# Two-layer masked attention: the closing turns and the opening's weight sums in another order

## The chip, the core and the metric

The kernel runs on one core of a Trainium2 chip. Its engines are TensorE (PE in the profile), VectorE (DVE), ScalarE (ACT), GpSimd (POOL) and SyncE (SP), which here issues all the transfers. Each engine works through its own queue of instructions in order, and waits by semaphores for what others must have done. The metric is the device time of one execution in microseconds (us).

## What is computed

The input x has 128 graphs of 128 nodes with 512 features, adj is a boolean mask for each graph. Two attention layers follow one another, each with a residual and a layer norm:

```python
# layer 0: 4 heads of 64
q, k, v = (split_heads(x @ W) for W in (Wq, Wk, Wv))
sim = where(adj, einsum(q, k) * 64 ** -0.5, -float32_max)
x = layernorm(x + einsum(softmax(sim), v) @ Wo + bo)
# layer 1: 8 heads of 64
h = (x - mean(x)) * rsqrt(var(x) + 1e-5) * gamma + beta
q, k, v = split(h @ w_qkv.T)
sim = where(adj | eye, einsum(q, k) * 64 ** -0.5, -1e9)
x = layernorm(x + einsum(softmax(sim), v) @ w_out.T + b_out)
```

All arithmetic is float32.

## The kernel before, in words

Graphs are taken in groups of two (G = 2), 64 groups in all (NG). The order of all instructions is written out by hand (`tc.manual_schedule()`, line 49): there is no scheduler, so the order of the calls in the functions is the order in every engine's queue. Pools of named tiles decide only which earlier use an instruction has to wait for.

The work is a software pipeline. A turn s of `step` (L819) makes for group s the first layer's q, k and v (`product_0`, L437), for group s-1 its scores and softmax, for s-2 its attention, output product and norm. For the second layer it makes q, k and v of group s-3 (`product`, called as `qk` and `v`), the softmax of s-4, and the attention, output product and norm of s-5. `opening` (L781) does turns 0 and 1, `step` runs for s = 2 to 63, `closing` for s = 64, 65 and 66, and `last` is turn 67.

Matrix products are made as seven block products in place of eight (numbered 1 to 7; the order is mostly 1, 2, 6, 5, 7, 3, 4). Three accumulation banks in PSUM, "a", "c" and "f", take them (`INTO`, L307). Products 1, 6, 7 and 4 all add into "a", so between two of them the partial result is read out: by ScalarE for 1, 6 and 5 (`tap`, L344, the copies `ev`, `eqk`, `e`), by VectorE with an add for 2, 7 and 3, and by ScalarE for 4. Each later product in the same bank waits for that read. In `out_product` (L476) every product is added to the residual rows `r` by VectorE (L501), and a next product in the same bank waits for that add.

The block products need sums of weight blocks, made once: `weight_sums` (L173) and `combine` (L182), four subtractions for each block, on VectorE but for one block of w1qk. They need sums of input blocks too: `halves_sums` (L296), four GpSimd operations for each group (`xs` of the input, `so` of the attention result).

A product wants the input with its features on the partitions. `turn` (L224) does that by way of DRAM: VectorE turns 32x32 blocks (L229), SP stores them (`scr`, L214), `arrive` (L233) fetches them with four transfers (`raw`, L220), and ScalarE puts them in order: `in_order` (L250) for layer 0, `finish` (L259), which applies gamma and beta, for layer 1. The probabilities go the same way: `normalised` (L582: a reciprocal on VectorE, a multiplication on GpSimd), `blocks` (L600: VectorE, then a store `scrp`), `probs_arrive` (L612: four fetches `pT`). In the opening and in the last turn `transposed` and `blocks_direct` (L621) have TensorE turn them instead. `finish_direct` (L274) would do so for the second layer's input; in the kernel before nothing calls it.

The softmax is `scores` (TensorE), `masked` (VectorE copies the scores under the mask into a tile that GpSimd has cleared), `maxima` (VectorE), `exps` (ScalarE, eight per part) and `normalised`. Part 0 is layer 0, parts 1 and 2 are the two graphs of layer 1. `attend` (L635) is probabilities times v, followed by a ScalarE copy (`aT`). `stats` (L684) makes mean and variance on VectorE, small GpSimd operations turn them into scale and shift, and the norms on ScalarE (L724) are put off to the next `flush()`. `addend` (L672) scales the residual rows on ScalarE (layer 1) and adds the bias on GpSimd (L679). `with_self` (L540) joins the diagonal to the mask. For the first two and the last three groups (`PLAIN_QK`) q and k of layer 1 are made with the features on the partitions at once.

Of the kernel before, what the change touches and what calls it, by code (L numbers as in the profile page):

```python
# [27 lines left out]
def kernel(ctx: ExitStack, tc: tile.TileContext, x, adj, wq, wk, wv, wo, bo,  # L28
                            gamma, beta, w_qkv, w_out, b_out, out):
    nc = tc.nc  # L30
    B, N, E = x.shape
    KC = E // P
    NG = B // G
# [136 lines left out]
    wsqk = const.tile([P, 3, KH, I1], F32, name="wsqk")  # L170
    wsv = const.tile([P, 3, KH, I1 // 2], F32, name="wsv")

    def weight_sums(w, ws, *blocks_):  # L173

        for c in blocks_:
            h0, h1 = (1, 0) if w is w1qk else (0, 1)
            b11, b12 = w[:, c, h0], w[:, c, h1]
            b21, b22 = w[:, KH + c, h0], w[:, KH + c, h1]
            combine(b11, b12, b21, b22, ws[:, 0, c], ws[:, 1, c], ws[:, 2, c],
                    eng=nc.gpsimd if w is w1qk and c == 0 else nc.vector)  # L180

    def combine(b11, b12, b21, b22, t2, t3, t4, eng=nc.vector):  # L182

        for o, a, b in ((b12, b12, b11), (t2, b22, b12), (t3, t2, b11), (t4, b21, t2)):
            eng.tensor_tensor(o, a, b, op=ALU.subtract)

    def weight_sums_0():
# [319 lines left out]
    PARTS = (0, 1, 2)  # L507
# [2 lines left out]
        g = s - (4 if part else 1)  # L510
        return g if 0 <= g < NG else None

    def scores(s):

        made = {}
        for part in PARTS:
# [302 lines left out]
    def step(s):  # L819

        made = scores(s)
        load_ahead(s + 1)
        if s > 2:
            in_order(s)
        if s > 3:
            sums(0, s)
        arrive(1, s - 3)
        flush()
        load_rows(s - 1)
        masked(made, s, 0, 1, 2)  # L830
        attend(s)
        maxima(s, 0, 1)
        out_sums(0, s - 2)
        if s == 3:
            sums(0, s)
        exps(s, 0, 0)
        product_0(s, 1)
        exps(s, 0, 1)
        out_product(0, s - 2, 1, 2, 5)
        maxima(s, 2)  # L840
        product_0(s, 2)
        normalised(s, 0)
        out_product(0, s - 2, 6, 3)
        exps(s, 1, 0)
        stats(0, s - 2, 0)
        if s == 2:
            turn(0, s + 1)
            arrive(0, s + 1)
        product_0(s, 6)
        exps(s, 1, 1)  # L850
        out_product(0, s - 2, 7)
        (blocks_direct if s == 2 else blocks)(s, 0)
        product_0(s, 5)
        out_product(0, s - 2, 4)
        normalised(s, 1)
        finish(s - 3, 0)
        stats(0, s - 2, 1)
        exps(s, 2, 0)
        product_0(s, 7)
        finish(s - 3, 1)  # L860
        exps(s, 2, 1)
        blocks(s, 1)
        product_0(s, 3)
        if s > 2:
            turn(0, s + 1)
        product_0(s, 4)
        if s in (2, 3):
            prepare(len(setup) - (s == 2))
        normalised(s, 2)
        if s == 3:  # L870
            weight_sums(w1v, wsv, 0, 1)
        qk(s - 3, 1)
        if s == 2:
            weight_sums(w1qk, wsqk, 1)
            prepare(1)
        flush()
        if s > 2:
            probs_arrive(s, 0, 1)
        qk(s - 3, 2)
        blocks(s, 2)  # L880
        qk(s - 3, 6, 5)
        flush(latest)
        addend(1, s - 5)
        out_sums(1, s - 5)
        qk(s - 3, 7, 3, 4)
        q_arrive(s - 3)
        k_arrive(s - 3)
        probs_arrive(s, 2)
        if s > 2:
            arrive(0, s + 1)  # L890
        out_product(1, s - 5, 1, 2)
        v(s - 3, 1, 2)
        turn(1, s - 2)
        cleared(s + 1, 0, 1, 2)
        v(s - 3, 6)
        out_product(1, s - 5, 6, 5)
        v(s - 3, 5)
# [8 lines left out]
        with_self(s - 2)  # L906
        if s == 3:
            weight_sums_out(1)
        if s == NG - 1:
            arrive(1, s - 2)  # L910

    def closing(s):

        chunks = [lambda p=p, i=i: exps(s, p, i) for p in PARTS if group_of(s, p) is not None
                  for i in range(2)]

        def some():
            if chunks:
                chunks.pop(0)()

        made = scores(s)
        flush()
        load_rows(s - 1)
        finish(s - 3, 0)
        masked(made, s, 0, 1, 2)
        attend(s)
        maxima(s, 0, 1)
        out_sums(0, s - 2)
        finish(s - 3, 1)
        out_product(0, s - 2, 1, 2)  # L930
        if s == NG + 2:
            addend(1, s - 5)
            out_sums(1, s - 5)
            out_product(1, s - 5, 1, 2)
        some()
        qk(s - 3, 1)
        maxima(s, 2)
        out_product(0, s - 2, 5, 6)
        some()
        qk(s - 3, 2)  # L940
        out_product(0, s - 2, 7, 3)
        if s == NG + 2:
            out_product(1, s - 5, 5, 6)
        some()
        qk(s - 3, 6)
        out_product(0, s - 2, 4)
        normalised(s, min(s - NG, 1))
        stats(0, s - 2, 0)
        stats(0, s - 2, 1)
        some()  # L950
        qk(s - 3, 5)
        blocks(s, min(s - NG, 1))
        some()
        qk(s - 3, 7)
        if s == NG:
            normalised(s, 1)
        some()
        flush()
        turn(1, s - 2)
        if s == NG + 2:  # L960
            normalised(s, 2)
            blocks(s, 2)
            probs_arrive(s, 1, 2)
            out_product(1, s - 5, 7, 3, 4)
        else:
            addend(1, s - 5)
            out_sums(1, s - 5)
        qk(s - 3, 3, 4)
        if s < NG + 2:
            if s == NG:  # L970
                blocks(s, 1)
            normalised(s, 2)
            out_product(1, s - 5, 1, 2)
            blocks(s, 2)
            probs_arrive(s, 0, 1, 2)
            arrive(1, s - 2)
            v(s - 3, 1, 2, 6)
            out_product(1, s - 5, 6, 5)
            v(s - 3, 5)
            out_product(1, s - 5, 7, 3, 4)  # L980
            v(s - 3, 7, 3, 4)
        flush(latest)
        stats(1, s - 5, 0)
        stats(1, s - 5, 1)
        cleared(s + 1, 0, 1, 2)
        addend(0, s - 1)
        with_self(s - 2)

    def last():
# [2 lines left out]
        made = scores(s)  # L992
        masked(made, s, 1)
        maxima(s, 1)
        v(s - 4, 1, 2, 6)
        exps(s, 1, 0)
        attend(s)
        flush()
        masked(made, s, 2)
        maxima(s, 2)  # L1000
        addend(1, s - 5)
        exps(s, 1, 1)
        out_product(1, s - 5, 1, 2)
        exps(s, 2, 0, 1)
        out_sums(1, s - 5)
        normalised(s, 1)
        addend(1, s - 4)
        v(s - 4, 5)
        out_product(1, s - 5, 6, 5)
# [20 lines left out]
    opening()  # L1030
    for s in range(2, NG):
        step(s)
    for s in range(NG, NG + 3):
        closing(s)
    last()


# [27 lines left out]
```

## Time and profile before

| what | us |
|---|---|
| median of 3 runs (2791.12 to 2794.29) | 2791.74 |
| the profiled execution | 2794.32 |
| its span | 2792.5 |
| TensorE busy | 2748.1 (98%) |
| VectorE busy | 1950.3 (70%) |
| GpSimd busy | 1748.8 (63%) |
| ScalarE busy | 1528.3 (55%) |
| share of TensorE in the chain of waits that ended last | 94% |
| turn 62, scores to scores (a steady turn) | 42.4 |
| turn 3 / turn 4 | 39.5 / 38.4 |
| turns 64, 65, 66 | 40.6, 40.3, 34.6 |
| from the scores of turn 67 to the end | 42.5 |

Times in the profile count from the start of the span. TensorE's busy time includes matmuls whose ends are modelled and overlap their successors, so what counts is the distance between starts. In a list of waits, the bracket at the end of a line gives the engine's idle time before that instruction and what ended it.

### The profile page before, as it was taken

The page shows a single profiled execution, that of the slowest core. Times are in us where ns is not written, and L with a number is a line of the kernel's source. Part 1 is how long each engine was busy: PE and PEld are TensorE (multiplying, and loading weights), DVE is VectorE, ACT ScalarE, POOL GpSimd, SP SyncE. Part 2 cuts the span into 40 slices and gives each one's busy share as a digit, 9 for nine tenths or more (in the row PEclk, how much of TensorE's full clock was granted, in tenths as well). Part 3 has the DMA queues.
Part 4 walks back from the last instruction along what each step waited for, and adds up shares of the span by engine and source line. Part 5 has one row for each costly group of instructions (what it writes and reads, how often), then busy time and mean ns, then how long its engine had stood idle before and what let it go on. Part 6 is the DMA issues. An engine that isn't in the chain of part 4 may idle for free.

```text
span 2792.5 us, 53773 instructions
## 1 busy us (share of the span) xinstructions
PE 2748.1 (98%) x18337; PEld 2184.7 (78%) x18337; DVE 1950.3 (70%) x3533; ACT 1528.3 (55%) x4869; POOL 1748.8 (63%) x2311
## 2 busy tenths in 40 slices
PE   8999999999999999999999999999999999999987
PEld 8878778778777787787787787787777877877876
DVE  5677677677677676776776776776776777767654
ACT  4465465565565564564654655655655645646534
POOL 5566666666666666666666666666666666666554
PEclk9999999999999999999999999999999999999999
DMA  5567777877777778778777777777777787787641
GB/s 169 145 193 209 219 209 209 217 209 214 215 209 219 210 208 221 206 206 226 207 207 223 206 209 218 209 217 211 208 218 210 210 225 203 206 222 210 167 120 54
DMA packets 474624, 563.52 MB, mean 202 GB/s; under 512 B 52200, under 2 KB 367600, under 8 KB 474352
## 3 DMA queue, kind: packets, MB, share of 16 engines
q1 hardware_dynamic: 474352, 560.09, 71.2%
q8 instruction: 147, 2.41, 0.4%
q14 instruction: 125, 1.02, 0.1%
HBM read 300.42 MB, written 259.52 MB: 201 GB/s over the span
## 4 chain that ended last, share of the span: by engine, by line
PE 94%; POOL 2%; issue 1%; DVE 1%; DMA 1%; ACT 1%; SPq 0%; POOLq 0%; DVEq 0%; ACTq 0%
PE qka L338 15%; PE a L459 12%; PE oa L497 11%; PE va L338 8%; PE qkf L338 8%; PE f L459 6%; PE av L658 6%; PE of L497 6%; PE qkc L338 4%; PE vf L338 4%; PE c L459 3%; PE oc L497 3%; PE sc L530 2%; PE sc L535 2%; PE vc L338 2%; PE sc_a L535 2%
## 5 line engine op out<-in xcount | busy, mean ns | idle before, releaser
L579 ACT ACTIVATE sm<-sm,nmax 128x128 f32<-128x128 f32 x1536 | 595.8, 395 | 14.1 <-DVE nmax L570 13.8
L588 POOL TENSOR_TENSOR sm<-sm,rec 128x1024 f32<-128x1024 f32 x192 | 364.2, 1897 | 288.4 <-DVE rec L587 288.4
L679 POOL TENSOR_TENSOR r<-r,bias 128x1024 f32<-128x1024 f32 x128 | 301.4, 2354 | 148.6 <-ACT r L678 148.6
L501 DVE TENSOR_TENSOR r<-oa,r 128x256 f32<-128x256 f32 x508 | 212.3, 418 | 190.3 <-PE oa L497 140.1
L579 ACT ACTIVATION_READ_ACCUMULATOR sm<-sm,nmax 128x1 f32 x1536 | 298.5, 194 | 0.0
L347 ACT COPY ev<-va 128x256 f32<-128x256 f32 x128 | 47.6, 372 | 441.4 <-PE va L338 440.1
L698 POOL TENSOR_SCALAR ve<-mv 128x2 f32<-128x2 f32 x191 | 41.4, 217 | 385.9 <-DVE mv L691 375.3
L606 DVE STREAM_TRANSPOSE turnedp<-sm 128x1024 f32<-128x1024 f32 x188 | 233.3, 1241 | 52.6 <-POOL sm L588 47.8
L302 POOL TENSOR_TENSOR xs<-xT 128x256 f32<-128x256 f32 x256 | 187.6, 733 | 115.7 <-ACT xT L256 92.5
L570 DVE TENSOR_REDUCE nmax<-sm 128x8 f32<-128x1024 f32 x192 | 226.5, 1206 | 0.2
L338 PE MATMUL qka<-wsqk,xs 128*128 128x512 f32 x472 | 221.8, 592 | 0.0
L338 PE MATMUL qkf<-w,xs 128*128 128x512 f32 x472 | 221.8, 592 | 0.0
L497 PE MATMUL oa<-wso,so 128*128 128x256 f32 x760 | 208.6, 384 | 11.8 <-DVE r L501 7.0
L497 PE MATMUL of<-wo,so 128*128 128x256 f32 x760 | 207.9, 382 | 3.1 <-POOL so L302 2.7
L724 ACT ACTIVATE r<-r,shift,root 128x512 f32<-128x512 f32 x254 | 192.7, 807 | 9.4 <-POOL shift L713 9.4
L564 DVE COPY_PREDICATED sm<-m,sc 128x512 f32<-128x512 uint8 x256 | 173.0, 730 | 10.6 <-PE sc L530 2.9
L338 PEld LDWEIGHTS qkf<-w,xs 128*128 128x128 f32 x472 | 89.7, 190 | 112.9 <-issue 112.9
L338 PEld LDWEIGHTS qka<-wsqk,xs 128*128 128x128 f32 x472 | 89.7, 190 | 112.9 <-issue 98.8
L690 DVE BATCH_NORM_STATS2 st<-r 128x6 f32<-128x512 f32 x254 | 174.8, 688 | 2.3
L550 POOL MEMSET sm<- 128x1024 f32 x192 | 174.9, 951 | 0.0
L497 PEld LDWEIGHTS of<-wo,so 128*128 128x128 f32 x760 | 144.6, 191 | 25.0 <-POOL so L302 4.0
L302 POOL TENSOR_TENSOR so<-aT 128x256 f32<-128x256 f32 (+1 forms) x254 | 150.7, 593 | 9.9 <-ACT aT L661 9.9
(178 smaller groups left out, 6797.7 us busy)
## 6 DMA issues: line engine op xcount, KB each, us to landing
scrp<-turnedp SPq DMA_DIRECT2D x188, 512.0 KB, 3.2
scr<-turned SPq DMA_DIRECT2D x125, 512.0 KB, 3.0
raw<-scr SPq DMA_DIRECT2D x500, 128.0 KB, 3.9
pT<-scrp SPq DMA_DIRECT2D x248, 256.0 KB, 4.8
r<-in_x_dram SPq DMA_DIRECT2D x63, 512.0 KB, 3.7
out_dram<-r SPq DMA_DIRECT2D x63, 512.0 KB, 3.5
x<-in_x_dram SPq DMA_DIRECT2D x61, 512.0 KB, 5.8
pT<-scrp SPq DMA_DIRECT2D x244, 128.0 KB, 4.2
```

What stands on the lines that cost most here:

```text
L302: nc.gpsimd.tensor_tensor(o, a0, a1, op=op)
L338: nc.tensor.matmul(o, lhsT, rhs, start=first and m == 0, stop=m == len(todo) - 1, skip_group_check=True)
L459: nc.tensor.matmul(acc[:, at * P:(at + 1) * P], lhsT, rhs, start=first and n == 0, stop=n == len(todo) - 1, skip_group_check=True)
L497: nc.tensor.matmul(acc, left[:, c], right[:, c], start=first and c == 0, stop=c == hk - 1, skip_group_check=True)
L501: nc.vector.tensor_add(part, acc, part)
L550: nc.gpsimd.memset(sm, NEG1 if part else NEG0)
L570: nc.vector.tensor_reduce(NMAX[part], SM[part], AX.X, ALU.max, negate=True)
L579: nc.scalar.activation(sm[:, i, k, :], sm[:, i, k, :], AF.Exp, bias=nmax[:, i, k:k + 1], accum_out=total[:, i, k:k + 1])
L588: nc.gpsimd.tensor_tensor(SM[part], SM[part], rec[:, :, :, None].to_broadcast([P, 2, K1, N]), op=ALU.mult)
L606: nc.vector.transpose(t.rearrange("p q (h r) -> p q h r", r=32), SM.pop(part).rearrange("p i k (q r) -> p q (i k) r", r=32))
L679: nc.gpsimd.tensor_tensor(R[g], R[g], (bias0, bias1)[l][:, None, :].to_broadcast([P, G, E]), op=ALU.add)
L724: nc.scalar.activation(R[g][:, b], R[g][:, b], AF.Identity, bias=shift[:, b:b + 1], scale=root[:, b:b + 1])
```

## The change

The diff makes two groups of edits. The first is in turns 2, 3 and 4. The four subtractions for the second block of w1qk, in turn 2 before, are made one at a time in turn 3 (`steps`). The sums of w1v go behind q and k products 6 and 7 of turn 3, and those of wo1 from the end of turn 3 into turn 4. The turning of group 0 for layer 1, with its fetches and its mask, moves from the end of turn 2 into turn 3; the input of group 3 is put in order at the end of turn 2; product 5 of v goes ahead in turns 3 and 4; output product 5 in turn 2 goes behind a product.

The second replaces `closing` by `closing_a` (turn 64) and `closing_b` (turns 65 and 66). There v of group s-4 is made at the start of the turn instead of v of group s-3 at its end; groups 62 and 63 are turned by TensorE (`finish_direct`) and no longer by way of DRAM; scores, exps, output products and the fetches of probabilities stand in another order. In `last`, two of v's products and a flush move.

```diff
-    def weight_sums(w, ws, *blocks_):
+    def weight_sums(w, ws, *blocks_, steps=range(4)):
...
-        for o, a, b in ((b12, b12, b11), (t2, b22, b12), (t3, t2, b11), (t4, b21, t2)):
+        todo = ((b12, b12, b11), (t2, b22, b12), (t3, t2, b11), (t4, b21, t2))
+        for o, a, b in (todo[i] for i in steps):
             eng.tensor_tensor(o, a, b, op=ALU.subtract)
...
-        if s > 2:
+        if s > 3:
             in_order(s)
-        if s > 3:
             sums(0, s)
-        arrive(1, s - 3)
+            arrive(1, s - 3)
         flush()
         load_rows(s - 1)
         masked(made, s, 0, 1, 2)
+        if s == 3:
+            turn(1, s - 3)
+            arrive(1, s - 3)
         attend(s)
         maxima(s, 0, 1)
         out_sums(0, s - 2)
         if s == 3:
             sums(0, s)
+            with_self(s - 3)
...
-        out_product(0, s - 2, 1, 2, 5)
+        out_product(0, s - 2, 1, 2, *(() if s == 2 else (5,)))
         maxima(s, 2)
         product_0(s, 2)
         normalised(s, 0)
-        out_product(0, s - 2, 6, 3)
+        out_product(0, s - 2, *((5,) if s == 2 else ()), 6, 3)
...
+        if s == 3:
+            weight_sums(w1qk, wsqk, 1, steps=(0,))
         product_0(s, 6)
...
         (blocks_direct if s == 2 else blocks)(s, 0)
+        if s == 3:
+            weight_sums(w1qk, wsqk, 1, steps=(1,))
         product_0(s, 5)
...
         stats(0, s - 2, 1)
+        if s == 3:
+            weight_sums(w1qk, wsqk, 1, steps=(2,))
...
         product_0(s, 3)
+        if s == 3:
+            weight_sums(w1qk, wsqk, 1, steps=(3,))
...
-        if s == 3:
-            weight_sums(w1v, wsv, 0, 1)
         qk(s - 3, 1)
         if s == 2:
-            weight_sums(w1qk, wsqk, 1)
             prepare(1)
+            in_order(s + 1)
...
-        qk(s - 3, 6, 5)
+        qk(s - 3, 6)
+        if s == 3:
+            weight_sums(w1v, wsv, 0)
+        if s == 4:
+            weight_sums_out(1)
+        qk(s - 3, 5)
...
+        if s < 5:
+            v(s - 3, 5)
         out_product(1, s - 5, 1, 2)
         v(s - 3, 1, 2)
-        turn(1, s - 2)
+        if s > 2:
+            turn(1, s - 2)
...
-        if s == 3:
-            weight_sums_out(1)
...
-    def closing(s):
...
+    def closing_a():
+
+        s = NG
+        made = scores(s, 1, 2)
+        attend(s, 0)
+        masked(made, s, 1, 2)
+        out_sums(0, s - 2)
+        finish(s - 3, 0)
+        attend(s, 1, 2)
+        made = scores(s, 0)
+        maxima(s, 1)
+        out_product(0, s - 2, 1, 2)
+        masked(made, s, 0)
+        finish(s - 3, 1)
+        out_product(0, s - 2, 5, 6)
+        maxima(s, 2)
+        flush()
+        load_rows(s - 1)
+        exps(s, 1, 0)
+        qk(s - 3, 1)
+        out_product(0, s - 2, 7, 3, 4)
+        qk(s - 3, 2)
+        stats(0, s - 2, 0)
+        stats(0, s - 2, 1)
+        maxima(s, 0)
+        exps(s, 1, 1)
+        qk(s - 3, 6)
+        addend(1, s - 5)
+        out_sums(1, s - 5)
+        exps(s, 2, 0)
+        qk(s - 3, 5)
+        normalised(s, 1)
+        out_product(1, s - 5, 1, 2)
+        flush()
+        exps(s, 2, 1)
+        qk(s - 3, 7)
+        blocks(s, 1)
+        out_product(1, s - 5, 5, 6)
+        normalised(s, 2)
+        flush(latest)
+        exps(s, 0, 0)
+        qk(s - 3, 3)
+        blocks(s, 2)
+        probs_arrive(s, 1, 2)
+        out_product(1, s - 5, 7, 3)
+        exps(s, 0, 1)
+        normalised(s, 0)
+        out_product(1, s - 5, 4)
+        qk(s - 3, 4)
+        cleared(s + 1, 1, 2)
+        addend(0, s - 1)
+        addend(1, s - 4)
+        stats(1, s - 5, 0)
+        stats(1, s - 5, 1)
+        with_self(s - 2)
+
+    def closing_b(s):
+
+        only = s == NG + 1
+        made = scores(s, 1, 2)
+        masked(made, s, 1, 2)
+        v(s - 4, 1, 2)
+        maxima(s, 1)
+        exps(s, 1, 0)
+        v(s - 4, 6, 5)
+        if only:
+            blocks(s - 1, 0)
+            probs_arrive(s - 1, 0)
+        maxima(s, 2)
+        flush()
+        v(s - 4, 7, 3, 4)
+        exps(s, 1, 1)
+        attend(s, 1, 2)
+        out_sums(1, s - 5)
+        finish_direct(s - 3)
+        exps(s, 2, 0)
+        out_product(1, s - 5, 1, 2)
+        normalised(s, 1)
+        attend(s, 0)
+        out_sums(0, s - 2)
+        qk(s - 3, 1)
+        out_product(1, s - 5, 5, 6)
+        exps(s, 2, 1)
+        qk(s - 3, 2)
+        blocks(s, 1)
+        out_product(1, s - 5, 7, 3)
+        normalised(s, 2)
+        qk(s - 3, 6)
+        out_product(1, s - 5, 4)
+        out_product(0, s - 2, 1, 2)
+        qk(s - 3, 5)
+        blocks(s, 2)
+        probs_arrive(s, 1, 2)
+        out_product(0, s - 2, 5, 6)
+        stats(1, s - 5, 0)
+        stats(1, s - 5, 1)
+        out_product(0, s - 2, 7, 3, 4)
+        qk(s - 3, 7)
+        stats(0, s - 2, 0)
+        stats(0, s - 2, 1)
+        cleared(s + 1, 1, 2)
+        flush()
+        qk(s - 3, 3, 4)
+        flush(latest)
+        addend(1, s - 4)
         with_self(s - 2)
...
-        v(s - 4, 1, 2, 6)
+        v(s - 4, 1)
+        attend(s)
         exps(s, 1, 0)
-        attend(s)
-        flush()
         masked(made, s, 2)
         maxima(s, 2)
-        addend(1, s - 5)
         exps(s, 1, 1)
         out_product(1, s - 5, 1, 2)
         exps(s, 2, 0, 1)
         out_sums(1, s - 5)
         normalised(s, 1)
+        v(s - 4, 2, 6)
...
-    for s in range(NG, NG + 3):
-        closing(s)
+    closing_a()
+    closing_b(NG + 1)
+    closing_b(NG + 2)
     last()
```

`finish_direct`, which was there and is called now, has in short:

```python
for b in range(G):
    pt = mm_tile(f"ht{g}_{b}")
    for c in range(KC):
        nc.tensor.transpose(pt[:, c * N:(c + 1) * N], R[g][:, b, c * P:(c + 1) * P], ident)
    ...  # scale by gamma, add beta: four ScalarE (b == 0) or four VectorE (b == 1) operations
sums(1, g)
```

More of the change, by code (lines that the diff above doesn't have):

```diff
@@ L179, in weight_sums, with combine @@
             combine(b11, b12, b21, b22, ws[:, 0, c], ws[:, 1, c], ws[:, 2, c],
-                    eng=nc.gpsimd if w is w1qk and c == 0 else nc.vector)
-    def combine(b11, b12, b21, b22, t2, t3, t4, eng=nc.vector):
-        for o, a, b in ((b12, b12, b11), (t2, b22, b12), (t3, t2, b11), (t4, b21, t2)):
+                    eng=nc.gpsimd if w is w1qk and c == 0 else nc.vector, steps=steps)
+    def combine(b11, b12, b21, b22, t2, t3, t4, eng=nc.vector, steps=range(4)):
+        todo = ((b12, b12, b11), (t2, b22, b12), (t3, t2, b11), (t4, b21, t2))
+        for o, a, b in (todo[i] for i in steps):
             eng.tensor_tensor(o, a, b, op=ALU.subtract)
@@ L511, in group_of, with scores @@
         return g if 0 <= g < NG else None
-    def scores(s):
+    def scores(s, *parts):
         made = {}
-        for part in PARTS:
+        for part in parts or PARTS:
             g = group_of(s, part)
@@ L884, in step @@
         out_sums(1, s - 5)
-        qk(s - 3, 7, 3, 4)
+        qk(s - 3, 7)
+        if s == 3:
+            weight_sums(w1v, wsv, 1)
+        qk(s - 3, 3, 4)
         q_arrive(s - 3)
@@ L896, in step @@
         out_product(1, s - 5, 6, 5)
-        v(s - 3, 5)
+        if s > 4:
+            v(s - 3, 5)
         out_product(1, s - 5, 7, 3, 4)
@@ L905, in step @@
         v(s - 3, 4)
-        with_self(s - 2)
-        if s == 3:
-            weight_sums_out(1)
+        if s > 2:
+            with_self(s - 2)
         if s == NG - 1:
             arrive(1, s - 2)
-    def closing(s):
[L914 to L921, printed above, removed]
+    def closing_a():
[13 more added lines that the diff above has]
+        maxima(s, 2)
@@ L922, in closing @@
         flush()
         load_rows(s - 1)
-        finish(s - 3, 0)
-        masked(made, s, 0, 1, 2)
-        attend(s)
[L927 to L931, printed above, removed]
-            addend(1, s - 5)
-            out_sums(1, s - 5)
-            out_product(1, s - 5, 1, 2)
-        some()
+        exps(s, 1, 0)
         qk(s - 3, 1)
-        maxima(s, 2)
-        out_product(0, s - 2, 5, 6)
-        some()
+        out_product(0, s - 2, 7, 3, 4)
@@ L940, in closing @@
         qk(s - 3, 2)
[L941 to L947, printed above, removed]
         stats(0, s - 2, 0)
         stats(0, s - 2, 1)
-        some()
+        maxima(s, 0)
[4 more added lines that the diff above has]
+        exps(s, 2, 0)
         qk(s - 3, 5)
-        blocks(s, min(s - NG, 1))
@@ L953, in closing @@
-        some()
+        normalised(s, 1)
+        out_product(1, s - 5, 1, 2)
+        flush()
+        exps(s, 2, 1)
         qk(s - 3, 7)
-        if s == NG:
-            normalised(s, 1)
-        some()
-        flush()
[L959 to L981, printed above, removed]
-        flush(latest)
+        blocks(s, 1)
+        out_product(1, s - 5, 5, 6)
+        normalised(s, 2)
@@ L983, in closing @@
+        flush(latest)
+        exps(s, 0, 0)
[10 more added lines that the diff above has]
+        addend(1, s - 4)
         stats(1, s - 5, 0)
         stats(1, s - 5, 1)
-        cleared(s + 1, 0, 1, 2)
-        addend(0, s - 1)
+        with_self(s - 2)
+    def closing_b(s):
[43 more added lines that the diff above has]
+        flush()
+        qk(s - 3, 3, 4)
+        flush(latest)
+        addend(1, s - 4)
@@ L994, in last @@
         maxima(s, 1)
-        v(s - 4, 1, 2, 6)
+        v(s - 4, 1)
+        attend(s)
         exps(s, 1, 0)
-        attend(s)
-        flush()
         masked(made, s, 2)
         maxima(s, 2)
-        addend(1, s - 5)
         exps(s, 1, 1)
```

## The prediction

> **What bounds the kernel.** I read the page first (TensorE busy 98% of the span, 94% of the chain of waits), then the busy time of each engine turn by turn. A turn is one pass of the loop over s; 3 and 4 are the first with second-layer work, 62 is a steady one, 64 to 66 are the closing turns and 67 the last.
>
> ```profile
> 56.90:96.40 39.50, 35.90 (x271) 33.06 (x270) 25.76 (x47) 15.52 (x40) 20.03 (x26) 0.96 0.36 108
> 96.40:134.80 38.40, 36.11 (x305) 33.47 (x304) 25.86 (x45) 19.60 (x69) 21.31 (x27) 1.00 0.60 165
> ...
> 2592.10:2634.50 42.40, 42.40 (x281) 33.23 (x280) 29.32 (x55) 23.79 (x76) 27.23 (x36) 1.00 0.70 192
> 2634.50:2675.10 40.60, 35.75 (x281) 31.92 (x280) 24.00 (x45) 20.52 (x69) 19.44 (x28) 0.96 0.35 111
> 2675.10:2715.40 40.30, 32.88 (x263) 30.04 (x262) 20.78 (x42) 17.67 (x53) 21.64 (x30) 1.00 0.36 94
> 2715.40:2750.00 34.60, 26.22 (x205) 24.29 (x204) 14.61 (x28) 13.96 (x46) 14.94 (x17) 0.90 0.33 87
> 2750.00:2792.50 42.50, 30.71 (x202) 25.16 (x200) 19.51 (x39) 16.82 (x51) 17.13 (x22) 0.91 0.20 59
> ```
>
> The columns are length, busy time of TensorE, its weight loads, VectorE, ScalarE, GpSimd, then granted clock and DMA. The steady turn (third row) has no idle TensorE. So nothing can be won in 59 of the turns; all that the change can move lies in the first two rows and the last four. TensorE idles there 3.6, 2.3, 4.9, 7.4, 8.4 and 11.8 us (6.3 of the last is the output's tail). Then I took TensorE's timeline for where, and what at a low clock.
>
> ```profile
> 65.93 0.67 PE L497 MATMUL oa<-wso,so 128*128 128x256 f32 x2 [2.08 <-DVE r L501]
> 67.72 2.05 PE L459 MATMUL a<-xs,ws 128*128 128x128 f32 x8 [0.26 <-ACT e L468]
> ...
> 2668.05 1.73 PE L497 MATMUL oa<-wso,so 128*128 128x256 f32 x4 [2.50 <-DVE r L501]
> 2680.53 1.09 PE L658 MATMUL av<-pT,qkv 128*64 128x128 f32 x16 [3.38 <-DMA pT<-scrp]
> 2720.34 3.25 PE L658 MATMUL av<-pT,v 128*64 128x128 f32 x32 [2.83 <-DMA pT<-scrp]
> 2765.16 2.07 PE L497 MATMUL oa<-wso,so 128*128 128x256 f32 x4 [4.18 <-POOL so L302]
> ```
>
> In brackets is the idle time and its releaser. Four output products (oa x4) take 0.86 from start to start when TensorE is full; at 2668 and 2765 they take about twice that, so a stall can be paid a second time at half clock. Summing gaps and slow stretches against full-rate pieces, the closing loses 6.9, 7.9, 11.8 and 8.5 us in 64 to 67 (35 in all, the tail not counted), turn 3 about 6.3, turn 4 about 3.2. The chain of waits says what makes the closing late.
>
> ```profile
> 2664.13 1.86 POOL sm L588
> 2666.06 1.13 issue
> 2667.19 0.10 DVE v L362
> 2667.29 3.17 DMA scrp<-turnedp
> ...
> 2673.74 9.77 DMA raw<-scr
> ```
>
> A turned block of probabilities or input goes out to DRAM and comes back before the next turn can attend or make q and k: 13 us from VectorE's end at 2667.3 to attention at 2680.5. Products with v are issued ahead of that wait, so nothing is left to cover it.
>
> **Closing, part by part.** I followed the new order along the rows above on the old clock (turn 64 starts at 2634.5), engine by engine. Work of TensorE in pieces, start to start: scores 1.0 per part, attention 0.93 per part, q-and-k product 1.79 (seven are 12.5), v or second-layer output product 0.86 (seven are 6.0), first-layer output product 0.43.
>
> Turn 64 loses its v (6.0 us), which goes to 65. Removed are two turns of the input (1.4 us of VectorE each), two 512 KB stores, eight fetches on SP's queue and eight ScalarE copies; so the 9.8 and 5.6 us landings of raw leave the path. Added are 16 turning matmuls (0.11 each by the opening's row L245, 1.7 us in all, wholly on TensorE). Their copies out of PSUM have no exact row: VectorE's 128x128 scale-and-shift lies between 0.1 and 0.55 (the 128x512 one, L764); I take 0.25, four of which are 1 us beside ScalarE's four. In turn 65 TensorE is then waiting for a block anyway, in 66 there are 0.8 us of slack; the bounds are -0.6 to +1.2 a turn in engine time and nothing on the path at the low end.
>
> Turn 64: first-layer attention, scores and four small products now run while the raw input is landing (2640.3), so the old 1.75 stall is filled; q and k follow at 2642.1. But GpSimd's queue decides next: ScalarE's ratio scaling ends at 2651.4, the bias takes 2.35 (to 2653.8), four sums 2.9 (2656.7), the normalisation 1.9 (2658.6), VectorE's turning 1.25 (2659.9). Adds of output products 5 and 6 stand behind that turning on VectorE, and product 7 needs the bank: stall 2.4. The second normalisation and turning repeat it: 2.0 before product 4. With 0.6 earlier, 5.1 lost; the turn ends at 2667.2. Old: 2675.1 less v is 2669.1. Gain 1.9.
>
> Turn 65: v of the group before covers the scores' maxima and exps. Scores end at 2669.2; VectorE's four masked copies (0.62 each), one v add and the maximum (1.15) end at 2672.7, and the copy of v's product 6 stands behind the four exps (1.55) that ScalarE has begun there, until 2674.6. V's product 7 adds into that bank and was ready at 2672.7: stall 2.0. Probabilities of parts 1 and 2 were turned by 2664.0; with 10 to 13 us of round trip they land at 2674 to 2677, and attention comes at 2677.3, so hidden; were v not there it would cost 8. Part 0 is turned only at 2673.8; 3.2 out, 1.75 to issue, 4.2 to land gives 2683: stall about 1. Both layers' output products now share one bank, so a product waits for the add before it, and adds stand behind a turning or two statistics (1.56): 0.7, 0.65, 1.1; the attention's copy by ScalarE, 0.45. Lost 5.9, work 33.2 (scores 2.0, v 6.0, attention 2.8, turning 0.9, q and k 12.5, output 9.0), end near 2706.5 against the old 2715.4 less v, 2709.4.
>
> Turn 66: the key copy waits behind two norms on ScalarE, and part 2's scores for it, 1.25; the copy of v's product 6 again 1.95; the attention's copy 0.4. Work 29.3, so it ends at 2739.6 (old: 2750.05; the old last v is made in turn 67 in both). Last turn: probabilities turned at 2734.05 plus 10.3 (old: 2745.0 to 2755.3) are there at 2744.3, stall 1.75; aT 1.25; tap 0.35. Three v products now cover the sums, where 4.2 stood. The last head's attention starts at 2760.1 instead of 2775.9; behind it nothing is changed. Closing: 15.8 gained.
>
> **Opening.** Turns from 5 on issue the same instructions in the same order, so they keep their length. Turn 2: product 5 moves behind a product, which removes a 0.74 wait, but the add behind it now stands behind a reciprocal that waits for exps (45.4): 0.3 worse. Turn 3: without 4.3 us of sums and the turn of the layer-one rows ahead of it, VectorE masks at once; reading the DMA'd input in order ahead of the norms on ScalarE lets TensorE start 0.4 earlier but ends the norms of group 0 at 60.3, which their turning on VectorE waits for (0.6), with the maximum behind it. The first adds come at 62.6 instead of 65.4, and the 2.1 stall with its half-clock stretch (1.3) goes. Given back: four sums in turn 3 (0.69 each, 2.8) push adds that TensorE waits for: 0.9 before product 4 and 1.0 before the last. Moving v's product 5 ahead avoids the wait for a key copy, 0.83. Net 3.4. On SP's queue the store and fetches of that turned block now follow the loads of the next input instead of preceding them; the block lands near 70, and q and k ask for it at 74.7. Turn 4: output weight sums (2.75) leave the head of the turn, so its gaps (1.25, and about 1.1 of small ones) and another 0.83 go: 3.3. They now stand between q-and-k adds that have 1.5 us of slack. Opening 6.4.
>
> [...] The row first:
>
> ```profile
> 56.90 2.32 DVE L185 TENSOR_TENSOR w<-w 128x512 f32<-128x512 f32 x1
> 59.25 0.69 DVE L185 TENSOR_TENSOR wsqk<-w 128x512 f32<-128x512 f32 x1
> ```
>
> The first sum took 2.3 us, ending when GpSimd's bias row did. [...] by the other rows, three in four are free. I take one collision, in the 0.9 above.
>
> The clock: granted 0.90 in turn 66, after stalls of 2 to 3 us. [...] by the rows half of those over 2 us were, at 1.3 to 2.7 (the three product groups from 2668.05 took 4.36 for 2.59). I go by the rows: one such stretch, 1.8.
>
> Sum: 6.4 + 15.8 - 1.8 = 20.4. The profiled execution took 2794.3 (span 2792.5), 0.09% above the median; so 2773.9 there and 2771 as a median.
>
> **Rivals.** (a) Waits that I counted as new do not appear, because blocks return sooner or ScalarE is not held: half of the closing's 18 us of stalls goes, 2762. For it: new waits are often near ties. Against: VectorE, ScalarE and GpSimd take work strictly in order in every row. 20%. (b) The closing only moves its stalls: each turn still attends behind a DRAM trip and in-order adds, a third of the closing's gain and the opening's come, 2780. For it: turn 64 gains but 1.9 by my own sum. 20%. (c) The opening alone works, [...] and the closing ends level: 2787. 4%. (d) Slower: the clock. Stalls split into more and shorter ones, twelve of at least 0.6 by my sum, and each is paid again at half clock; at 1.85 a stretch it takes 12 stretches to eat the 22 and 15 to lose 0.2%: 2798. Before had five. 4%. My forecast, 2766 to 2776: 52%.
>
> Range 2760 to 2781: it holds the forecast and most of (a) and (b). A measurement tells about 0.2%, 5.6 us, from no change: faster 0.92, same 0.04, slower 0.04.
>
> **Signs.** Right if turn 4 has almost no idle TensorE and turn 3 under 3, if attention of turns 65 and 66 (parts 1 and 2) waits for no DMA, if output product 7 in turn 64 waits for VectorE by 2 to 3 us, and if v's third product waits for ScalarE. Wrong if raw or part 0's block still holds TensorE over 3 us, or the clock falls below 0.9 over a whole turn.

## The result and the profile after

| | before | after |
|---|---|---|
| median of four runs, us | 2793.01 (2791.12 to 2794.98) | 2775.90 (2775.42 to 2776.21) |
| ratio | | 0.9939, 95% interval 0.9921 to 0.9956 |
| the profiled execution / its span | 2794.32 / 2792.5 | 2776.21 / 2774.4 |
| TensorE busy | 2748.1 (98%) | 2744.8 (99%) |

The change saves 17.1 us; 20.4 were forecast. By turns, each counted from its first scores (after, TensorE's timeline has them at 37.24, 56.54, 93.35, 129.72, 2628.56, 2663.83, 2703.42 and 2737.09, and the last head's attention at 2757.66):

| stretch | before | after | difference | forecast |
|---|---|---|---|---|
| turn 2 | 19.04 | 19.30 | +0.3 | +0.3 |
| turn 3 | 39.54 | 36.81 | -2.7 | -3.4 |
| turn 4 | 38.34 | 36.37 | -2.0 | -3.3 |
| turns 5 to 63 | 2499.7 | 2498.8 | -0.8 | 0 |
| turn 64, v's 6.0 left out before | 34.6 | 35.3 | +0.7 | -1.9, and 1.8 of clock |
| turn 65 (v in both) | 40.4 | 39.6 | -0.8 | -1.1 |
| turn 66 with v after, without before (+6.0) | 40.6 | 33.7 | -7.0 | -7.5 |
| turn 67 to the last head's attention | 25.9 | 20.6 | -5.3 | -5.4 |

These are the same two groups of turns as before, busy time turn by turn (length, TensorE, weight loads, VectorE, ScalarE, GpSimd, clock, DMA share and rate):

```profile
56.50:93.30 36.80, 34.86 (x272) 31.71 (x270) 22.95 (x46) 15.58 (x40) 19.75 (x26) 1.00 0.34 102
93.30:129.70 36.40, 35.87 (x303) 33.23 (x302) 25.30 (x45) 19.59 (x69) 21.11 (x27) 1.00 0.61 170
2628.50:2663.80 35.30, 31.73 (x251) 28.05 (x250) 21.49 (x44) 18.83 (x65) 21.95 (x31) 0.90 0.28 84
2663.80:2703.40 39.60, 35.06 (x271) 30.58 (x270) 21.94 (x44) 16.89 (x53) 18.86 (x26) 1.00 0.44 114
2703.40:2737.10 33.70, 30.26 (x243) 27.49 (x242) 16.55 (x31) 16.40 (x52) 18.35 (x25) 1.00 0.17 54
2737.10:2774.40 37.30, 27.82 (x201) 23.28 (x200) 17.75 (x37) 15.41 (x49) 14.15 (x16) 0.97 0.23 66
```

TensorE idles 1.9 and 0.5 us in turns 3 and 4 (3.6 and 2.3 before), and 3.6, 4.5, 3.4 and 9.5 in the closing (4.9, 7.4, 8.4, 11.8). The clock row has changed places: 0.96, 0.90 and 0.91 in turns 64, 66 and 67 became 0.90 in turn 64 and 0.97 in 67 (there only behind TensorE's last product: up to 2767.5 the row is 1.00). TensorE's timeline of after says what the idle time waits for now:

```profile
68.41 0.70 PE L498 MATMUL oa<-wso,aT 128*128 128x256 f32 x2 [0.53 <-DVE r L502]
72.45 1.16 PE L460 MATMUL a<-xT,ws 128*128 128x128 f32 x8 [0.67 <-DVE qkv L474]
...
90.56 1.13 PE L339 MATMUL va<-wsv,xs 128*128 128x256 f32 x4 [0.46 <-ACT ev L348]
...
2655.32 1.10 PE L498 MATMUL oa<-wso,so 128*128 128x256 f32 x4 [2.38 <-DVE rec L588]
2656.26 1.75 PE L498 MATMUL of<-wo,so 128*128 128x256 f32 x4
...
2658.90 2.07 PE L498 MATMUL oa<-wso,aT 128*128 128x256 f32 x4 [0.88 <-DVE r L502]
...
2671.53 1.13 PE L339 MATMUL va<-wsv,xs 128*128 128x256 f32 x4 [2.00 <-ACT ev L348]
...
2680.75 2.05 PE L339 MATMUL qka<-xT,w 128*128 128x128 f32 x16 [0.69 <-ACT aT L662]
...
2742.35 1.97 PE L659 MATMUL av<-pT,v 128*64 128x128 f32 x32 [2.15 <-DMA pT<-scrp]
```

The waits of 3.38 and 2.83 for probabilities are gone from turns 65 and 66: no attention there waits for a transfer. So is the 4.18 for GpSimd's sums near the end. In their place stand product 7 of the second layer's output behind VectorE (2.38), v's third product behind ScalarE (2.00, and 1.98 again in turn 66), and one trip by DRAM that is left, in turn 67. The chain of waits, where 13 us of such a trip lay before turn 65, has now only this last one:

```profile
2736.43 5.79 DMA pT<-scrp
2742.22 0.14 issue
2742.35 1.97 PE av L659 x32
```

### The profile page after: what moved, and what is told of

Same layout as the page of the kernel before. It is cut to its first block, busy times and chain, and to the rows that moved or that the text cites. A ratio compares the mean times of both kernels' runs of the same rounds, so it can differ in the third digit from the quotient of the medians.

```text
span 2774.4 us, 53786 instructions
## 1 busy us (share of the span) xinstructions
PE 2744.8 (99%) x18353; PEld 2180.9 (79%) x18353; DVE 1945.2 (70%) x3537; ACT 1526.4 (55%) x4869; POOL 1748.5 (63%) x2311
## 4 chain that ended last, share of the span: by engine, by line
PE 96%; DVE 1%; ACT 1%; POOL 1%; issue 0%; DMA 0%; SPq 0%; POOLq 0%; ACTq 0%; DVEq 0%
PE qka L339 16%; PE a L460 13%; PE oa L498 12%; PE va L339 8%; PE qkf L339 8%; PE av L659 6%; PE f L460 6%; PE of L498 6%; PE qkc L339 4%; PE vf L339 4%; PE c L460 3%; PE oc L498 3%; PE sc L531 2%; PE sc L536 2%; PE vc L339 2%; PE sc_a L536 2%
```

## The experiments

The theory at this point: both halves work as forecast, and the closing's gain is what is left after new waits, each behind an engine that takes its queue in order; a stall may be paid again at half clock, as the 2.38 of turn 64 was (behind it the granted clock was 0.50 from 2658 to 2662). Its rivals: the gain comes from one part alone (TensorE's turning of the input, say), the new place of v is worth no more than the old one, or the new waits stand for nothing, since another wait would come up behind them. Ratios are to the kernel before on the same chip, with 95% intervals. Distances from after are between medians, and those of before were not alike beside them: 2793.01 beside after, 2794.99 to 2795.72 beside experiments 1 to 10. So each such distance is uncertain by some 2 us, and for smaller differences the traces decide.

**1. opening_only**: turns 2 to 4 of after, `closing` and `last` of before.

```diff
-    closing_a()
-    closing_b(NG + 1)
-    closing_b(NG + 2)
+    for s in range(NG, NG + 3):
+        closing(s)
```

> The opening's edits alone, with closing and last turn as before. By the walk corrected with the trace after (turn 2 longer by 0.3, turn 3 shorter by 2.7, turn 4 by 2.0): 4 to 5 us below the kernel before. [...]

Measured: 2790.28, ratio 0.9983 (0.9976 to 0.9990), so -4.8 us. The opening gives what its turns show.

**2. closing_only**: the other half; `step` and `weight_sums` of before.

```diff
-        if s > 3:
+        if s > 2:
             in_order(s)
...
+            weight_sums(w1qk, wsqk, 1)
```

> The closing's edits alone, with the opening as before. If the two halves add: 12 to 13 us below the kernel before, and with the other half they make the whole 17. If most of the gain were the opening's: under 6.

Measured: 2780.81, ratio 0.9949 (0.9935 to 0.9964), -14.3 us, a little more than expected. The halves add: 4.8 + 14.3 = 19.1 against 17.1, within the intervals.

**3. adds_first**: in turn 64, the adds of output products go ahead of the turnings of probabilities on VectorE. TensorE's own order is the same.

```diff
-        blocks(s, 1)
         out_product(1, s - 5, 5, 6)
         normalised(s, 2)
+        blocks(s, 1)
...
+        out_product(1, s - 5, 7, 3)
         blocks(s, 2)
         probs_arrive(s, 1, 2)
-        out_product(1, s - 5, 7, 3)
```

> After, with turn 64's adds of output products 5 and 6, and 7 and 3, ahead of the turnings of probabilities on VectorE, and the second normalisation asked for earlier; TensorE's order is unchanged. Theory (adds behind a turning stall product 7, and the stall brings the half clock): the 2.4 stall and the slow stretch in turn 64 go, turn 64 from 35.3 to about 30.5, 4 to 5 us below the kernel after. Rival (the blocks of probabilities decide, so the time comes back as a wait for their fetch in turn 65): 0 to 2 us below.

Measured: 2772.69, ratio 0.9920 (0.9905 to 0.9935), 3.2 below after (4 to 5 were expected; by the ratios it is 5.3, and the two intervals overlap). What the adds stood behind is to be read in VectorE's timeline of after:

```profile
2653.29 1.25 DVE L607 STREAM_TRANSPOSE turnedp<-sm 128x1024 f32<-128x1024 f32 x1 [3.29 <-POOL sm L589]
2654.46 0.38 DVE L502 TENSOR_TENSOR r<-of,r 128x256 f32<-128x256 f32 x1
2654.77 0.41 DVE L502 TENSOR_TENSOR r<-oa,r 128x256 f32<-128x256 f32 x1
2655.10 0.18 DVE L588 RECIPROCAL rec<-total 128x8 f32<-128x8 f32 x1
```

VectorE sat idle for 3.29 us at the head of its queue, waiting for GpSimd's multiplication, with two adds ready behind. In adds_first, product 7 no longer waits, and product 4, the next in its bank, keeps a part of its own wait:

```profile
2655.87 1.13 PE L498 MATMUL oa<-wso,aT 128*128 128x256 f32 x4 [0.84 <-DVE r L502]
```

Its turn 64 is 29.8 us long, against 33.2 of after where no half clock comes in (again_b, below). The later turning of probabilities cost nothing: no attention of turn 65 waits for a transfer. The gain in the whole is smaller than in the turn, since a half-clock stretch then stood in turn 65 (41.2 us, clock 0.96) instead of 64.

**4. taps_first**: in turns 65 and 66, v's products 6 and 5, and so ScalarE's copies of them, go ahead of the exps.

```diff
         maxima(s, 1)
-        exps(s, 1, 0)
         v(s - 4, 6, 5)
+        exps(s, 1, 0)
```

> After, with the copies of v's products 6 and 5 ahead of the four exps on ScalarE in turns 65 and 66. Theory: the two 2.0 us waits of v's product 7 go, and the exps are not late since their maximum ends at the same time: 2.5 to 3.6 us below the kernel after. Rival (the exps then end later and attention's sums wait as long): 0 to 1 us below.

Measured: 2772.57, ratio 0.9921 (0.9904 to 0.9937), 3.3 below after, as expected (5.0 by the ratios, with intervals that overlap too). Both waits of 2.0 for ScalarE are gone, and turns 65 and 66 together are 3.1 us shorter, with no half clock in either kernel there; a wait for VectorE's add takes part of the first one's place:

```profile
2670.72 1.13 PE L339 MATMUL va<-wsv,xT 128*128 128x256 f32 x4 [0.85 <-DVE v L363]
```

**5. input_by_dram**: the input of groups 62 and 63 by way of DRAM, as before, in the new order.

```diff
-        finish_direct(s - 3)
+        finish(s - 3, 0)
+        finish(s - 3, 1)
```

with `turn(1, s - 2)` and `arrive(1, s - 2)` in turns 64 and 65.

> After, with the input of groups 62 and 63 turned by VectorE and a DRAM trip again instead of by TensorE; v stays a turn behind. Theory (what counts is that v covers the trips; the turning by TensorE is worth little): between 1 us below and 3 us above the kernel after, with a wait for the fetched input at most in turn 66. Rival (the DRAM trip of the input was the bound of the closing): 6 to 12 us above.

Measured: 2777.31, ratio 0.9938 (0.9924 to 0.9953): after's time. TensorE's turning of the input is worth nothing that can be measured here.

**6. direct_only**: the reverse, the kernel before with `finish_direct` for those two groups and nothing else.

```diff
-        finish(s - 3, 0)
...
-        finish(s - 3, 1)
+        finish_direct(s - 3)
```

(in turns 65 and 66), with `turn(1, s - 2)` and `arrive(1, s - 2)` left out of `closing`.

> Before, with nothing changed but the input of groups 62 and 63 turned by TensorE. Theory (attention still waits for the probabilities' trip): 1 to 4 us below the kernel before. Rival (the input's trip was the bound): 6 to 12 us below.

Measured: 2795.87, ratio 1.0004 (0.9996 to 1.0013). No gain, where 1 to 4 us were expected: a miss. The attention of turn 65 starts when the probabilities land, however early TensorE gets there:

```profile
2680.91 1.97 PE L658 MATMUL av<-pT,qkv 128*64 128x128 f32 x16 [6.42 <-DMA pT<-scrp]
2682.64 3.65 PE L658 MATMUL av<-pT,v 128*64 128x128 f32 x32
```

Before, that line started at 2680.53 and had waited 3.38. The wait is 3.0 longer, but not because the edit saved as much: turn 64 started 1.4 earlier in this execution, and had no half clock, which cost before 1.8 there. Behind the wait the attention itself ran at half clock (3.65 for 1.97).

**7. v_at_end**: after, but v in turns 64 and 65 at the turn's end, in the old place (v of group s-3).

```diff
     def closing_a():
...
+        v(s - 3, 1, 2, 6, 5, 7, 3, 4)
...
     def closing_b(s):
-        v(s - 4, 1, 2)
...
-        v(s - 4, 6, 5)
...
-        v(s - 4, 7, 3, 4)
...
+        if only:
+            v(s - 3, 1, 2, 6, 5, 7, 3, 4)
```

> After, with v made at the end of turns 64 and 65 for the group of that turn, as before, instead of at the start of the next; all other order as in the kernel after. Theory (v's six us of products now cover masks, maxima and exps of the next scores, which start six us earlier): 4 to 8 us above the kernel after. Rival (only the cover of the DRAM trip counts, and that is the same in either place): within 2 us of it.

Measured: 2785.71, ratio 0.9968 (0.9955 to 0.9981), 9.8 above after (8.1 by the ratios), somewhat more than expected: without its new place for v, the new order keeps only the smaller part of the closing's gain. Some 5 us of this trace (an estimate from the distances between starts) are half clock behind its three longest stalls, 5.18, 3.75 and 2.55 us, where after has 2.1; without either, some 6 us remain. But it is not the DRAM trip that the new place covers; v covers that at the turn's end as well. SyncE's queue shows when the fetches for turn 65 are asked for, in before and, below it, in v_at_end:

```profile
2670.53 1.75 SPq L220 DMA_DIRECT2D pT<-scrp  x4
```

```profile
2661.62 1.75 SPq L221 DMA_DIRECT2D pT<-scrp  x4
```

In before this is 4.6 us ahead of the turn's first scores (2675.09), all three parts together. In v_at_end parts 1 and 2 go ahead of part 0, and their fetch is 6.9 us ahead (2668.47), with all of v behind it; the attention at 2670.45 doesn't wait. No run changes that order alone. What is late here is ScalarE's copy of the attention, which stands behind exps that wait for scores, mask and maxima:

```profile
2673.51 0.40 ACT L580 ACTIVATE sm<-sm,nmax 128x128 f32<-128x128 f32 x1 [4.57 <-DVE nmax L571]
...
2678.01 1.04 ACT L664 COPY aT<-av 128x512 f32<-128x512 f32 x2
```

```profile
2678.63 2.08 PE L498 MATMUL oa<-wo,aT 128*128 128x256 f32 x4 [5.18 <-ACT aT L664]
...
2725.74 1.74 PE L498 MATMUL oa<-wo,aT 128*128 128x256 f32 x4 [3.75 <-ACT aT L664]
```

**8. sums_together**: after, but the four subtractions for w1qk in one piece at the end of turn 2.

```diff
+            weight_sums(w1qk, wsqk, 1)
             prepare(1)
...
-        if s == 3:
-            weight_sums(w1qk, wsqk, 1, steps=(0,))
```

and likewise for steps 1 to 3.

> After, with the four sums of w1qk's second block made together at the end of turn 2, as before, instead of one by one in turn 3. Theory: turn 3's masks and adds come up to 4 us later, TensorE waits about 2 more: 1.5 to 3 us above the kernel after. Rival (the sums cost the same stalls wherever they stand): within 0.5 us of it.

Measured: 2777.65, ratio 0.9935 (0.9919 to 0.9952); the times can't tell it from after, but the trace can. Turn 3 is 39.2 us long instead of 36.8, within what was expected. The old wait of turn 3 is back, and the turn's v product 7 comes at 93.07 instead of 90.56:

```profile
65.89 0.67 PE L498 MATMUL oa<-wso,so 128*128 128x256 f32 x2 [2.45 <-DVE r L502]
```

**9. filler**: after, with 20 turning matmuls of the unit matrix, which nothing reads, ahead of the stalled product 7 in turn 64. It asks whether the half clock behind that stall goes when TensorE isn't idle.

```diff
+        pt = mm_tile("filler")
+        for _ in range(5):
+            for c in range(KC):
+                nc.tensor.transpose(pt[:, c * P:(c + 1) * P], ident, ident)
         out_product(1, s - 5, 7, 3)
```

> After, with 20 turning matmuls of the unit matrix (about 2.2 us of TensorE, nobody reads them) put ahead of output product 7 in turn 64, where TensorE stands idle for 2.4 us. Theory [...]: product 3, product 4 and the next q-and-k product run at full rate, 2 to 3 us below the kernel after although work is added. Rival (they are slow for another reason, such as their operands or VectorE's reads): no faster, 0 to 0.5 us above.

Measured: 2776.79, ratio 0.9936 (0.9921 to 0.9950): no gain, a miss. Turn 64 had no half clock and took 33.2 us; but taps_first and v_at_end had none there either with the stall unfilled (2.39), and filler had two half-clock stretches elsewhere: behind the 2.01 wait of turn 65 (41.2 us instead of 39.6) and at the wait of turn 67 (2.44, then 3.63 for an attention of 1.97). By itself it decides nothing.

**10. combined**: adds_first and taps_first together, the key copy of turn 66 ahead of ScalarE's norms, and v's product 3 ahead of 7 in turns 3 and 4.

```diff
-        flush()
         qk(s - 3, 3, 4)
+        flush()
...
-        v(s - 3, 7)
+        v(s - 3, 3 if s < 5 else 7)
```

and the converse for the later one of the two.

> After, with four reorderings: the adds ahead of the turnings in turn 64, the copies of v's products ahead of the exps in 65 and 66, the key copy ahead of the norms in 66, and v's product 3 ahead of 7 in turns 3 and 4. If each stall seen in the trace after is its own: 4.5, 3, 1 and 1.2 us, together 8 to 10 us below the kernel after. If they give way to one another (the fetch of probabilities next): 4 to 6.

Measured: 2768.74, ratio 0.9908 (0.9891 to 0.9924), 7.2 below after (8.7 by the ratios), between the two expectations: the fastest kernel of the study. Its clock was 1.000. The swap in turns 3 and 4 brought nothing: product 3 now covers ScalarE's copy of 6, but product 4, directly behind 7, waits for VectorE's add of 7 instead:

```profile
92.67 1.13 PE L339 MATMUL va<-wsv,xT 128*128 128x256 f32 x4 [0.52 <-DVE v L363]
```

The trip of turn 67 is still there (2.20).

**11 and 12. again_a, again_b**: after, unaltered, in two more executions.

> The changed kernel once more, unaltered. It asks whether the half clock behind the 2.4 us stall in turn 64 belongs to this program or to the moment of the execution. [...] the stall of 2.38 us is there again at the same place, product 3 and product 4 of the output take 1.03 each or 1.75 and 2.07 by chance, and the turn is 33.2 or 35.3 us long. If it belongs to the program's own pattern of work (rival), the turn is 35.3 again in each execution, with 1.75, 2.07 and 3.13 as before.

> The same kernel a third time, for the same question: by the theory the two repeats and the first profile need not agree on the half clock, in turn 64 (33.2 or 35.3 us) or in the attention of the last turn (1.97 or about 3.5 us); by the rival all three show the same stretches.

Measured: 2773.67 and 2776.04. TensorE's timeline of again_a, and below it of again_b, behind the same stall:

```profile
2654.97 1.42 PE L498 MATMUL oa<-wso,so 128*128 128x256 f32 x4 [2.39 <-DVE rec L588]
2656.18 1.91 PE L498 MATMUL of<-wo,so 128*128 128x256 f32 x4
...
2658.55 1.35 PE L498 MATMUL oa<-wso,aT 128*128 128x256 f32 x4 [0.45 <-DVE r L502]
```

```profile
2655.90 1.10 PE L498 MATMUL oa<-wso,so 128*128 128x256 f32 x4 [2.38 <-DVE rec L588]
2656.84 1.03 PE L498 MATMUL of<-wo,so 128*128 128x256 f32 x4
...
2659.48 1.13 PE L498 MATMUL oa<-wso,aT 128*128 128x256 f32 x4 [1.61 <-DVE r L502]
```

With after's own timeline above, that is one stall in three executions of one program: in this order, half clock from 2656.3 to 2663 (granted 0.51 there), from 2655 to 2659 (0.50 from 2656 to 2658), and not at all (1.00 from 2654 to 2664). The turn took 35.3, 33.4 and 33.2 us. again_b had its stretch in turn 66, behind the 1.98 wait (35.3 us instead of 33.7). The rival, a pattern that belongs to the program, is refuted. The middle case also shows when a stretch is cheap: where half clock runs into a wait for another engine, that wait shrinks (1.61 to 0.45), and only 0.25 of 1.4 us is paid.

## Why the prediction was right, and where its terms were off

The mechanism held. The time lay inside the range, 4.9 us above the forecast; opening_only and closing_only measured each half apart, and the signs named ahead are there: turn 4 idles 0.5 us and turn 3 1.9; no attention of turns 65 and 66 waits for a transfer; product 7 waits 2.38 for VectorE (2.4 was worked out), v's third product 2.00 for ScalarE (2.0), the last turn's probabilities 2.15 (1.75).

Rivals: (a), that the new waits don't appear, is refuted by these lines; (c), the opening alone, by closing_only; (d), slower, by every run. (b), a closing that only moves its stalls, was too pessimistic: the closing gained 12.3 us by the turns, not a third of 15.8. But it names what took most of the rest, in turn 64.

The profiled executions are 18.1 us apart, so 2.3 of the 20.4 are missing between them (the medians are 17.1 apart; the runs of before alone scatter by 3.9). Term by term:

- *Opening, 4.4 us where 6.4 were forecast.* The step "moving v's product 5 ahead avoids the wait for a key copy, 0.83" counted only the wait that goes. Product 5 had also stood between 6 and 7 and covered ScalarE's copy of 6. Without it, product 7 waits 0.46, and the two products start 1.49 apart instead of 0.87: 0.62 given back in each turn, 1.2 in all. In turn 4 the "about 1.1 of small ones" were worth 0.5: of the three late output products (0.79, 0.86 and 0.59 behind the product before them; 0.43 is the pace), two came down to 0.45 and 0.66, and the third stayed, because they still start some 0.15 behind the end of VectorE's add in their bank (101.85 and 103.83, starts at 101.99 and 103.98). The swap in combined shows that the bank's other read, VectorE's of product 7, is as late as ScalarE's of 6: only another product between them covers either.
- *Turn 64.* Taken without half clock (33.2 in again_b, taps_first, filler), it is 0.5 over the 32.7 of the sum. The stalls were the ones worked out (2.38 and 1.61 in again_b for 2.4 and 2.0); the work between them was mis-sized, 28.9 for 27.6. The clock then cost 2.1 where 1.8 was allowed. The allowance, an estimate from the rows of before (by the prediction's count half of the stalls over 2 us were paid a second time at half clock there), was right as to size: the three executions paid 2.1 and 0.25 in turn 64 and 1.6 in turn 66. That the stretch fell into turn 64 in the profiled execution was a matter of chance.
- *Turns 65 and 66*, +0.3 and +0.6, are the balance of two errors. The stalls were smaller than forecast, 4.5 for 5.9 and 3.4 for 3.6: part 0's probabilities did not keep TensorE waiting (1 us expected), and the shared bank's waits were 0.52, 0.61 and 0.73 for 0.7, 0.65 and 1.1, against a copy of the attention of 0.69 for 0.45 and turn 66's key copy of 1.46 for 1.25. The work between was longer, 35.0 for 33.2 and 30.2 for 29.3. Much of that is how a bracket counts: v's products around the stall of 2.00 start 3.02 and 0.97 apart where 0.86 is the pace, so it cost 2.27. The sum priced its stalls as brackets and its work at full pace, and left out what lies between.
- Against these, 0.6 us ahead of turn 2 and 0.8 in turns 5 to 63 came in that no step had. The 0.6 is chance: three executions of after reach turn 2 at 37.24, 36.90 and 37.81. The 0.8 goes with the opening's edits: turns 5 to 63 take 2498.9 in opening_only, too, but 2499.7 in closing_only and 2499.9 in sums_together. Most of it lies in three turns, 26, 35 and 58, of 42.79, 42.44 and 42.69 us in before where others take 42.35. closing_only has the same three (42.83, 42.46, 42.69); in after none takes over 42.40. The profile names no wait there, and the cause stays open. So "turns from 5 on keep their length" was off by that much.

One sentence was wrong, though the number that hung on it was not: that products with v, issued ahead of the wait for probabilities, leave nothing to cover it, so that v in its new place hides the trip (8 us without). v_at_end puts v back and loses 8.7 us in the span, but behind ScalarE, not behind a transfer: v covers the trip in either place, once the fetch is asked for ahead of it. In its new place v covers the softmax of the same turn: mask, maxima and exps, which otherwise hold ScalarE's queue, and with it the copy of the attention. This was tried in the new order only; what v's move would give in the old one was not run. input_by_dram and direct_only add that taking the input's trip away is worth nothing where another chain is late.

The prediction allowed for one sum drawn out beside a GpSimd operation, in the 0.9 before product 4. The timelines of GpSimd and VectorE in after show the first two of the scattered sums and what ran beside them:

```profile
65.57 1.90 POOL L589 TENSOR_TENSOR sm<-sm,rec 128x1024 f32<-128x1024 f32 x1 [0.17 <-DVE rec L588]
67.18 0.84 DVE L186 TENSOR_TENSOR w<-w 128x512 f32<-128x512 f32 x1
...
69.43 0.65 DVE L186 TENSOR_TENSOR wsqk<-w 128x512 f32<-128x512 f32 x1
```

Only the first overlaps a GpSimd operation of full width (the normalisation, to 67.47), and it took 0.84; the others took 0.65, 0.66 and 0.68. That is 0.2 us here; product 4 waits 0.53 for its add, not 0.9. The sum of 2.32 us in before, from 56.90 to 59.22, did not end with GpSimd's bias operation, as the prediction reads it, but 0.56 behind it:

```profile
56.31 2.35 POOL L679 TENSOR_TENSOR r<-r,bias 128x1024 f32<-128x1024 f32 x1
```

In after the first sum ends 0.55 behind the normalisation. So both end that long behind GpSimd's operation, a little less than a sum takes with GpSimd idle (0.65, at 69.43). That a sum can take longer beside a wide GpSimd operation rests on these two rows; what held it is not shown.

## What to carry to other kernels

When a piece of work is moved to fill a gap, ask what it covered where it stood: product 5 of v gave 0.62 of its 0.83 us back because it had hidden a copy. In an engine that works in order, an instruction that waits at the head of the queue holds back ready ones behind it (two adds behind VectorE's 3.29 us in turn 64 of after); moving two small adds ahead of a turning (adds_first) or two copies ahead of exps (taps_first) gained about 3 us each (3.4 and 3.1 by the turns that they touch, half clock left out; the times alone are less clear), together more than a third of what the whole change did; the first left TensorE's order as it was, the second moved nothing but the exps. A DRAM trip is worth removing only where it is what comes last: that of the input made no difference in two kernels (input_by_dram, 2777.31 where after took 2775.90; direct_only, ratio 1.0004). And a stall can cost more than the bracket in the list of waits says (2.27 for 2.00 here), so a sum is better made from distances between starts.

## What the runs showed of the hardware that was not expected

The half clock behind a stall is not a property of the stall. Waits of 2.0 and 2.4 us were followed by half clock in some executions and by none in others of the same program (the three executions above), and before and opening_only had none behind a wait of 3.38. The wait of 2.00 at 2671.53 in after had none either; the same wait in adds_first (at 2666.43) was followed by a clock of 0.50 from 2668 to 2670. What decides it is not shown. The kept traces of the kernels with the new closing hold 35 waits of 1.8 to 2.4 us in turns 64 to 67. Half clock followed 12 of them and cost about 15 us in all by the lengths of the turns, so a wait of this kind is to be given an expected price of some 0.4 us (an estimate, 15 us over 35 waits; 0, 0.25 and 2.1 measured for one of them). Half clock followed all six waits of 3.7 us and more in turns 64 to 67 of the kept traces (3.75 in v_at_end to 6.42 in direct_only). Two kernels that differ by 2 us in one profile each are not told apart by it.
